# Experts' rows transposed by VectorE and sums fetched by token, in a four-layer kernel

## The chip, the cores and the metric

The kernel runs on one core of one Trainium2 chip, as one launch. The metric is device time in microseconds (us). A core has five engines that run their own instruction queues in order and wait for one another by semaphores: TensorE (PE in the profile: matmuls, with the weight loads shown apart as PEld), VectorE (DVE), ScalarE (ACT), GpSimd (POOL) and SyncE (SP, which here only issues transfers). Transfers run on 16 DMA engines, issued from the queues of SP, ACT and POOL.

## The reference

Two sequences of 1024 tokens, 512 features, all in fp32, pass four blocks, each with a layer norm in front and a residual sum behind: causal attention with 16 heads, a mixture of experts, a state space block, and a feed-forward block whose weights are entries of a table of 16 values.

```python
x = x + _L0_attn_ref(_layernorm(x, axis=-1), ...)
x = x + _L0_ffn_ref(_layernorm(x, axis=-1), ...)      # 32 experts of 192, 8 for a token
x = x + _L1_attn_ref(_layernorm(x, axis=-1), ...)     # state space block
x = x + _L1_ffn_ref(_layernorm(x, axis=-1), ...)      # w = lut[idx], inner size 1376

sel_w, sel_e = jax.lax.top_k(router_logits, TOP_K)
sel_w = jax.nn.softmax(sel_w.astype(jnp.float32), axis=1)
masked = jnp.zeros((T, E), dtype=jnp.float32).at[rows, sel_e].set(sel_w)
...
g = jnp.einsum('th,eih->tei', x, w_gate_proj)
u = jnp.einsum('th,eih->tei', x, w_up_proj)
h = jax.nn.silu(g) * u
h = h * masked_w[:, :, None]
out = jnp.einsum('tei,ehi->th', h, w_down_proj)
```

## The kernel before

Four stretches follow one another: attention (to about 780 us of the profiled span), the experts (to 1520), the state space block (to about 2290) and the feed-forward block.

**Rows and slots.** Beside attention `_Router.route` (L171) normalises blocks of 128 tokens, finds the eight experts of each token and gives each pair of token and expert a slot: each expert has 608 slots (`CAP`), four blocks of 128 and one of 96. `send` (L292) scatters, for one of the eight places and one block, 128 rows of 545 values (`ROW`: 512 features, the token's number, 32 weights) into the DRAM tensor `rows` by an indirect DMA on POOL. The slots are cleared beforehand by SP (`clear`, L400). `acc` is a pair of DRAM tensors in which the sums of tokens grow; the first starts as a copy of the input of the block, and `kept` holds a second copy for the rare case that an expert has no slots left (`_left_over`, L1267, which runs only then).

**Parts.** `_Experts` (L982) goes through the experts from the last to the first, each in two parts: a front part of two blocks (the first sequence) and a back part of three (128, 128, 96 rows). They alternate: front part of expert n, back part of expert n-1. For one part p the method `part` (L1172) writes down the order of TensorE, VectorE and ScalarE by hand (inside `manual_schedule`, L1869, these three engines keep the order of the program):

- `gates(p, 0)` (L1093): four matmuls with the first 128 columns of the expert's weights into a PSUM bank of tag `g`, then SiLU on ScalarE;
- `turn_block(p + 1, 0)` and `(p + 1, 1)` (L1081): for the next part, four TensorE transposes of a block into PSUM (`xg_ps`) and a copy by ScalarE into `xgT`;
- `down(p - 1)` (L1125): the down products of the part before, then ScalarE scales each block's sums by the token's weight into `y` (L1163) and POOL adds them to `acc` by an indirect, accumulating DMA (L1165), whose list of tokens `tok` VectorE copied out of the rows (L1078);
- `gates(p, 1)`, VectorE's product `hT` (L1113);
- `turn_block(p + 1, 2)` for the 96 rows of a back part;
- `gates(p, 2)`, a second SiLU, VectorE's products `hU` (L1121);
- `load_rows(p + 3)` (L1021): SP loads the rows of a later part into `xg`, one row a partition. Such a load waits for the sends that bring its rows.

fp32 matmuls appear as two records each in the profile; a transpose as one.

**Look-up.** Between these steps `rest` (L1217) takes steps of `_look_up` (L904), which turns the table indices of the feed-forward weights into weights in DRAM (`ffn_w`). A piece is 128 x 688 or 128 x 512 indices: SP loads it, ScalarE shortens int32 to bf16 (L927), and for each of the 16 values VectorE makes a mask (L943) and adds mask times value to the sum (L944); SP stores it. It starts at the sixth part.

**The state space block** (`_state_space`, L1347) goes through eight stages of 128 tokens of each sequence. `prepare(st)` (L1382) loads x and both sums from `acc`, adds them (L1393), normalises and transposes. `begin` (L1501) and `products` (L1563) do one chunk step k; POOL makes `xd` (L1528) and `cd` (L1538) for the matmuls of the step after. Outside `manual_schedule` a planner with costs of its own sets the order within each queue.

Of the kernel before, what the change touches and what calls it, by code (L numbers as in the profile page):

```python
# [8 lines left out]
F32 = mybir.dt.float32  # L9
I32 = mybir.dt.int32  # L10
U32 = mybir.dt.uint32
# [34 lines left out]
ROW = D + 1 + E  # L46
# [61 lines left out]

class _Router:
# [8 lines left out]
    def __init__(self, tc, g, x_sb, a, pool, rows, acc, kept, left, ready):  # L118
        nc = tc.nc
        self.tc, self.g, self.x_sb, self.kept = tc, g, x_sb, kept  # L120
        self.pool, self.rows, self.acc, self.left, self.ready = pool, rows, acc, left, ready
# [4 lines left out]
        nc.scalar.dma_start(out=self.wr, in_=a["wr"])  # L126
# [7 lines left out]
        self.number = pool.tile([P, NBLK], I32, tag="number", name="number")  # L134
        nc.gpsimd.iota(self.number, pattern=[[P, NBLK]], base=0, channel_multiplier=1)
# [35 lines left out]
    def route(self, blocks, wk, row_of, bank, apart=False):  # L171
# [12 lines left out]
        for to in (self.acc[0], self.kept):  # L184
            nc.sync.dma_start(
                out=to[b0 * P : (b0 + n) * P, :].rearrange("(n p) d -> p n d", p=P),
                in_=x_sb[:, b0 : b0 + n, :],
            )
# [6 lines left out]
        for i, blk in enumerate(blocks):  # L195
            row = row_of(blk)
            xr.append(row)
            nc.vector.tensor_scalar(
                row[:, :D], x_sb[:, blk, :], mv[:, i, 0:1], rstd[:, i : i + 1],
                ALU.subtract, ALU.mult,  # L200
            )
            nc.gpsimd.tensor_copy(row[:, D : D + 1], self.number[:, blk : blk + 1])
# [74 lines left out]
        for i in range(n):  # L277
            nc.vector.tensor_scalar(
                xr[i][:, D + 1 :], ex[:, i, :], den[:, i : i + 1], None, ALU.mult
            )  # L280
        yield

        nc.vector.tensor_tensor(chosen, chosen, valid, ALU.subtract)  # L283
        miss = wk.tile([P, n, E], F32, tag="miss", name="miss")
        for i in range(n):
            nc.vector.tensor_tensor(miss[:, i, :], chosen[:, i, :], xr[i][:, D + 1 :], ALU.mult)
# [41 lines left out]


def _attention(tc, g, x_sb, a, router, gates, load_gates, make_experts):  # L330


# [11 lines left out]
    rows, acc, ready = router.rows, router.acc, router.ready  # L344
    with ExitStack() as ctx:
# [47 lines left out]

        blank = rp.tile([P, ROW], F32, tag="row", name="blank")
        nc.gpsimd.memset(blank, 0.0)
        nob = wp.tile([P, 1], I32, tag="nob", name="nob")
        nc.gpsimd.iota(nob, pattern=[[0, 1]], base=NT, channel_multiplier=1)
        nc.gpsimd.tensor_copy(blank[:, D : D + 1], nob)

        def clear():  # L400
            for n in range(E * CAPB):
# [1582 lines left out]
```

## Time and profile before

| | us |
|---|---|
| median of 3 runs (2790.9 to 2794.2) | 2792.37 |
| the profiled execution, by the same clock | 2791.15 |
| its span, first to last instruction | 2789.4 |

The profile is of one execution, and its times count from the start of its span. An entry of "busy" is the time in which an engine had an instruction at work; "idle <- X" is what ended the wait before. Some groups of instructions in the experts' stretch, from 830 to 1520 us:

| line | what | count | mean us |
|---|---|---|---|
| L1088 | TensorE transpose of 128x128 | 472 | 0.273 (records overlap) |
| L1091 | ScalarE copy of a transposed block, 128x512 | 118 | 0.591 |
| L1163 | ScalarE scaling of a block's sums, 128x512 | 92 | 0.685 |
| L1165 | POOL, issue of an accumulating scatter | 155 | 1.705 |
| L297 | POOL, issue of a send | 36 | 1.045 |
| L943 | VectorE mask, 128x688 bf16 | 240 | 0.344 |
| L944 | VectorE mask times value plus sum, 128x688 | 240 | 0.936 |
| L927 | ScalarE shortening, 128x688 int32 | 16 | 0.761 |

The 40 slices of the span in tenths of busy time show the stretches (the experts lie in slices 12 to 22):

```
PE   7999999999998899999997899999999999999999
DVE  5555543555236799997774444455455452101100
ACT  1344432443433233333332344444344432101010
POOL 2222220334455533443343010111011010000000
DMA  3366532212479999998885211111111140000000
```

### The profile page before, as it was taken

How to read it: one execution, taken by the hardware profiler on the slowest of the kernel's cores; microseconds unless marked ns; L12 is line 12 of the kernel's file. 1: busy time of each engine (PE TensorE's matmuls, PEld its weight loads, DVE VectorE, ACT ScalarE, POOL GpSimd, SP SyncE). 2: the span in 40 equal slices, each digit the busy share in tenths (PEclk: the TensorE clock that was granted, in tenths of full speed). 3: DMA queues.
4: the chain of work that ended last, by engine and by line, in shares of the span. 5: the costliest groups of instructions: out<-in, count | busy, mean ns of one | idle time of the engine just before them, and what ended most of it. 6: DMA issues, size and time to landing. Idle time of an engine off the chain costs nothing. (4 is left out here: it accounts for less than half of the span.)

```text
span 2789.4 us, 34767 instructions
## 1 busy us (share of the span) xinstructions
PE 2674.8 (96%) x11976; PEld 1616.1 (58%) x11976; DVE 1428.9 (51%) x4016; ACT 925.9 (33%) x1886; POOL 635.4 (23%) x787
## 2 busy tenths in 40 slices
PE   7999999999998899999997899999999999999999
PEld 3444444544465566666664687777777774444444
DVE  5555543555236799997774444455455452101100
ACT  1344432443433233333332344444344432101010
POOL 2222220334455533443343010111011010000000
PEclk9999999999989999999999899999999999999999
DMA  3366532212479999998885211111111140000000
GB/s 116 112 196 188 162 118 76 80 65 82 154 246 251 241 231 256 258 245 200 209 196 93 65 20 43 31 43 43 36 37 49 31 158 15 26 12 23 30 0 27
DMA packets 241257, 311.28 MB, mean 112 GB/s; under 512 B 61264, under 2 KB 129872, under 8 KB 240304
## 3 DMA queue, kind: packets, MB, share of 16 engines
q1 hardware_dynamic: 207808, 232.64, 27.9%
q0 software_dynamic: 32256, 75.58, 12.7%
q8 instruction: 98, 1.61, 0.2%
q10 hardware_dynamic: 1008, 0.73, 0.1%
q14 instruction: 87, 0.71, 0.1%
HBM read 157.93 MB, written 150.95 MB: 111 GB/s over the span
## 5 line engine op out<-in xcount | busy, mean ns | idle before, releaser
L1100 PE MATMUL pg<-xgT,wgu 128*128 128x256 f32 (+1 forms) x1536 | 429.0, 432 | 20.1 <-DVE hT L1113 18.1
L1100 PEld LDWEIGHTS pg<-xgT,wgu 128*128 128x128 f32 x1536 | 289.1, 194 | 149.8 <-issue 56.1
L1165 POOL DMA_INDIRECT acc<-y,tok x160 | 272.0, 1700 | 381.7 <-DMA acc<-y,tok 98.7
L944 DVE SCALAR_TENSOR_TENSOR acc<-hit,lut,acc 128x688 f32<-128x688 bf16 (+2 forms) x405 | 348.8, 861 | 14.4
L1466 PE MATMUL pf<-xT,win 128*128 128x256 f32 x1024 | 245.1, 387 | 9.0 <-ACT gate L1494 4.1
L654 ACT ACTIVATE pT<-st 128x512 f32<-128x512 f32 (+3 forms) x384 | 158.0, 498 | 176.5 <-PE st L641 159.6
L549 PE MATMUL sp<-ka,qa 64*128 64x512 f32 (+3 forms) x768 | 206.9, 510 | 7.5 <-DVE mx L570 4.0
L1466 PEld LDWEIGHTS pf<-xT,win 128*128 128x128 f32 x1024 | 187.8, 191 | 43.0 <-PE pf L1466 7.4
L641 PE MATMUL st<-qa,ka 64*128 64x512 f32 (+3 forms) x768 | 177.3, 500 | 1.5 <-ACT qa L590 1.2
L570 DVE TENSOR_REDUCE mx<-sp 128x1 f32<-128x384 f32 (+3 forms) x352 | 167.3, 491 | 17.9 <-PE sp L549 10.7
L658 POOL TENSOR_SCALAR_AFFINE_SELECT pT<-pT 128x128 f32<-128x128 f32 x256 | 84.1, 341 | 380.6 <-ACT pT L654 369.1
L297 POOL DMA_INDIRECT rows<-row,idx x128 | 128.8, 1007 | 108.3 <-DVE chosen L283 43.6
L1774 PE MATMUL po<-wd,f_hT 128*128 128x512 f32 (+1 forms) x352 | 152.6, 592 | 0.0
L672 PE MATMUL y<-pT,v 128*64 128x512 f32 (+3 forms) x768 | 147.0, 516 | 2.1 <-ACT raw L609 2.0
L549 PEld LDWEIGHTS sp<-ka,qa 64*128 64x128 f32 x768 | 91.7, 186 | 93.5 <-issue 48.8
L1718 DVE TENSOR_TENSOR f_hT<-s,pu 128x512 f32<-128x512 f32 (+1 forms) x37 | 25.4, 687 | 231.4 <-PE pu L1712 231.4
L563 DVE CUSTOM_DVE_ANT_0 junk<-sp,cmask 128x128 f32<-128x128 f32 x256 | 73.2, 286 | 137.3 <-PE sp L549 136.9
L641 PEld LDWEIGHTS st<-qa,ka 64*128 64x128 f32 x768 | 100.1, 188 | 59.6 <-issue 32.4
L1163 ACT ACTIVATE y<-yo,rw 128x512 f32<-128x512 f32 (+1 forms) x128 | 80.8, 682 | 160.3 <-PE yo L1155 160.3
L1712 PE MATMUL pg<-f_xT,wg 128*128 128x512 f32 (+1 forms) x296 | 133.4, 593 | 0.0
L1538 POOL TENSOR_TENSOR cd<-ft_c,ec 128x256 f32<-128x256 f32 x56 | 40.8, 730 | 406.2 <-PE cb L1552 204.9
L1712 PE MATMUL pu<-f_xT,wu 128*128 128x512 f32 (+1 forms) x296 | 133.2, 592 | 0.0
(213 smaller groups left out, 4011.0 us busy)
## 6 DMA issues: line engine op xcount, KB each, us to landing
rows<-blank SPq DMA_DIRECT2D x160, 272.5 KB
xg<-rows SPq DMA_DIRECT2D x64, 545.0 KB
csb<-cs_rows SPq DMA_DIRECT2D x128, 128.0 KB
wgu<-in_wg_dram SPq DMA_DIRECT2D x32, 256.0 KB
wgu<-in_wu_dram SPq DMA_DIRECT2D x32, 256.0 KB
wd<-in_wd_dram SPq DMA_DIRECT2D x32, 256.0 KB
wd<-in_wd_dram SPq DMA_DIRECT2D x64, 128.0 KB
x<-x SPq DMA_DIRECT2D x32, 256.0 KB
```

What stands on the lines that cost most here:

```text
L297: t = tc.nc.gpsimd.indirect_dma_start(out=self.rows[:, :], out_offset=bass.IndirectOffsetOnAxis(ap=idx[:, i, k : k + 1], axis=0), in_=xr[i ...
L549: nc.tensor.matmul(sp[hh][:, c0:c1], lhsT=q[half, pr, tb * P : (tb + 1) * P], rhs=k[half, pr, k0 * P : k1 * P], start=True, stop=True,)
L570: nc.vector.tensor_reduce(m[:, n : n + 1], sp[hh][:, c0:c1], AX.X, ALU.max)
L641: nc.tensor.matmul(st[:, c0:], lhsT=k[half, j // 2, kb * P : (kb + 1) * P], rhs=q[half, j // 2, qt * 512 + c0 : (qt + 1) * 512], start=Tru ...
L654: e = nc.scalar.activation(pT[:, c0:], st[:, c0:], AF.Exp)
L672: nc.tensor.matmul(y[j // 2][half, c0:], lhsT=v[:, kb, h // 2, h % 2 : h % 2 + 2, :].rearrange("p k d -> p (k d)"), rhs=ps[j][:, c0:], sta ...
L944: nc.vector.scalar_tensor_tensor(acc, hit, lut[:n, k : k + 1], acc, ALU.mult, ALU.add)
L1100: nc.tensor.matmul(pg, lhsT=wgu[:, cc, m * P : (m + 1) * P], rhs=xgT[:, cc, :cols], start=cc == 0, stop=cc == NCC - 1,)
L1165: nc.gpsimd.indirect_dma_start(out=self.router.acc[to][:, :], out_offset=bass.IndirectOffsetOnAxis(ap=tok[:m, j : j + 1], axis=0), in_=y[: ...
L1466: nc.tensor.matmul(pf, lhsT=w[wn][:, cc, c0 : c0 + P], rhs=xT[st][:, cc], start=cc == 0, stop=cc == NCC - 1,)
L1712: nc.tensor.matmul(dst[:n, :], lhsT=w[:, cc, fc * P : fc * P + n], rhs=self.xT[tt][:, cc, :], start=cc == 0, stop=cc == NCC - 1,)
L1774: nc.tensor.matmul(po, lhsT=self.hT[tt][fc // 4][:n, fc % 4, j * P : (j + 1) * P], rhs=wd[:n, fc, :], start=fc == 0, stop=fc == NFC - 1,)
```

## The change

**Layout of a row.** A row has 544 values, without the token's number. Its 512 features stand in another order, quarter by quarter: feature c·128 + q·32 + f is stored at q·128 + c·32 + f. The router's weights are loaded in the same order by four transfers.

**Transposes.** `load_rows` brings a part's rows by four transfers, one for each quarter of the features, into 32 partitions each, so that blocks of 32 x 32 lie where VectorE's transpose can turn them into `xgT`. The token's weight for the expert comes by one or two more transfers of single values (`mark`). The gates get four PSUM banks in place of two and two for the transposes.

**Sums.** The scaled sums of a part are stored by SP in the order of the slots (`put`, DRAM tensor `ys`). Each token's eight slots are kept (`slots`), and its sums are fetched by indirect DMAs on POOL (`_collect`), accumulating from the second on: for the state space block's first stage during the last experts, for the second before its first step, for later stages two gathers a chunk step. `acc` is one tensor that is not added to, `kept` is gone.

**Look-up.** A piece is 344 or 256 columns wide. VectorE takes the four bits of the index apart, ScalarE makes eight leaves (the lower or the upper value of each pair of table entries, by the lowest bit), and seven predicated copies on VectorE choose among them by the other bits. Loads and stores of a piece are issued from ScalarE's queue. In each part from the sixth on, eight steps of it are taken: two, three, none and three after the four steps of `part`.

**Order.** The transposes stand after `down`, after `gates(p, 1)` and before `gates(p, 2)`; two places instead of three are sent ahead of the loop, and the third and fourth at its first two parts.

```diff
-ROW = D + 1 + E
+ROW = D + E
...
+def _by_quarter(row):
+    return row[:, :D].rearrange("p (q c f) -> p c q f", q=NQ, f=Q)
...
+        wr = a["wr"].rearrange("(q f) c e -> c f q e", f=Q)
+        for c in range(NCC):
+            nc.scalar.dma_start(out=self.wr[c * Q : (c + 1) * Q], in_=wr[c])
...
-        for to in (self.acc[0], self.kept):
-            nc.sync.dma_start(
-                out=to[b0 * P : (b0 + n) * P, :].rearrange("(n p) d -> p n d", p=P),
-                in_=x_sb[:, b0 : b0 + n, :],
-            )
+        nc.sync.dma_start(
+            out=self.acc[b0 * P : (b0 + n) * P, :].rearrange("(n p) d -> p n d", p=P),
+            in_=x_sb[:, b0 : b0 + n, :],
+        )
...
+                _by_quarter(row), x_sb[:, blk, :].rearrange("p (c q f) -> p c q f", q=NQ, f=Q),
+                mv[:, i, 0:1], rstd[:, i : i + 1], ALU.subtract, ALU.mult,
...
+        nc.vector.tensor_copy(self.slots[:, b0 : b0 + n, :], slot)
...
+        clearing = chain(
+            (rows[r : min(r + P, 1 + E * CAP), :] for r in range(1, 1 + E * CAP, P)),
+            (ys[r : r + P, :] for r in range(0, 1 + (TOPK - 1) * CAP, P)),
+        )
...
-    half = FI // 2
+    most = FI // 4
...
+            for part in range(4):
+                cols = slice(part * most, (part + 1) * most)
+                pieces.append((P, most, a[src][:, cc, cols], ffn_w[dst][:, cc, cols]))
+    for part in range(2):
+        cols = slice(part * D // 2, (part + 1) * D // 2)
+        for fc in range(NFC - 1):
+            pieces.append((P, D // 2, a["didx"][:, fc, cols], ffn_w["wd"][:, fc, cols]))
+        pieces.append((FTAIL, D // 2, a["didx_tail"][:, cols], ffn_w["wd_tail"][:, cols]))
...
-        nc.sync.dma_start(out=idx, in_=src)
+        idx = pool.tile([P, most], I32, tag="idx", name="idx")[:n, :width]
+        nc.scalar.dma_start(out=idx, in_=src)
...
-        short = pool.tile([P, half], BF16, tag="short", name="short", bufs=2)[:n, :width]
+        short = pool.tile([P, most], I16, tag="short", name="short")[:n, :width]
...
+    def store(dst, leaf, bits):
+        nc.scalar.dma_start(out=dst, in_=leaf[0])
+    def merge(leaf, bits, j, k):
+        nc.vector.copy_predicated(leaf[j], bits[k], leaf[j + (1 << k - 1)])
+    more = pool.tile([P, NLUT // 2], F32, tag="more", name="more")
+    pairs = lut.rearrange("p (j k) -> p k j", k=2)
+    nc.vector.tensor_tensor(more, pairs[:, 1], pairs[:, 0], ALU.subtract)
...
+        follows = pieces[i + 1] if i + 1 < len(pieces) else None
+        bits, leaf = [], {}
+        for k in range(4):
+            bit = pool.tile([P, most], I16, tag=f"bit{k}", name="bit", bufs=1 + (k == 3))
+            bits.append(bit[:n, :width])
+            nc.vector.tensor_scalar(
+                bits[k], short, k, 1, ALU.logical_shift_right, ALU.bitwise_and
...
+            )
+        if follows:
+            idx = load(*follows)
+        yield
...
+        def leaves(j):
+            for j in (j, j + 1):
+                tag, bufs = ("leaf", 4) if j else ("acc", 2)
+                leaf[j] = pool.tile([P, most], F32, tag=tag, name=tag, bufs=bufs)[:n, :width]
+                nc.scalar.activation(
+                    leaf[j], bits[0], AF.Identity,
+                    scale=more[:n, j : j + 1], bias=lut[:n, 2 * j : 2 * j + 1],
+                )
+        if done:
+            merge(*done[1:], 0, 3)
+        leaves(0)
+        yield
+        leaves(2)
+        merge(leaf, bits, 0, 1)
+        yield
+        if done:
+            store(*done)
+        merge(leaf, bits, 2, 1)
+        yield
+        leaves(4)
+        merge(leaf, bits, 0, 2)
+        yield
+        leaves(6)
+        merge(leaf, bits, 4, 1)
+        yield
+        if follows:
+            short = shorten(idx, *follows)
+        merge(leaf, bits, 6, 1)
+        yield
+        merge(leaf, bits, 4, 2)
+        yield
+        done = dst, leaf, bits
+    merge(*done[1:], 0, 3)
+    yield
+    store(*done)
...
+def _collect(nc, ys, slots, blk, k, to, add):
+    kw = {"compute_op": ALU.add} if add else {}
+    return nc.gpsimd.indirect_dma_start(
+        out=to, out_offset=None, in_=ys[:, :],
+        in_offset=bass.IndirectOffsetOnAxis(ap=slots[:, blk, k : k + 1], axis=0), **kw,
+    )
...
-        xg = self.wk.tile([P, CAPB - FRONTB, ROW], F32, tag="xg", name="xg", bufs=3)[:, :n]
+        most = CAPB - FRONTB
+        xg = self.wk.tile([P, most * NQ, P], F32, tag="xg", name="xg", bufs=3)
+        mark = self.wk.tile([P, most], F32, tag="mark", name="mark", bufs=5)
...
-        pieces = [(
-            xg[:, : n - back],
-            rows[r : r + (n - back) * P, :].rearrange("(n p) d -> p n d", p=P),
-        )]
+        pieces = [
+            (
+                xg[q * Q : (q + 1) * Q, : m // Q],
+                rows[r : r + m, q * P : (q + 1) * P].rearrange("(t r) d -> r t d", r=Q),
+            )
+            for q in range(NQ)
+        ]
+        c = D + e
+        pieces.append((
+            mark[:, : n - back],
+            rows[r : r + (n - back) * P, c].rearrange("(n p) -> p n", p=P),
+        ))
         if back:
             r += (n - 1) * P
-            pieces.append((xg[:LASTB, n - 1], rows[r : r + LASTB, :]))
+            pieces.append((mark[:LASTB, n - 1 : n], rows[r : r + LASTB, c : c + 1]))
...
+        self.turned[p] = self.wk.tile([P, NCC, most * P], F32, tag="xgT", name="xgT", bufs=2)
...
     def turn_block(self, p, j):
         if p >= len(self.order) or j >= self.blocks(p):
             return
-        nc, xg, xgT = self.tc.nc, self.xg[p], self.turned[p][0]
-        pt = self.bank("t", [P, NCC, P], "xg_ps")
-        m = self.of_block(p, j)
-        for cc in range(NCC):
-            nc.tensor.transpose(
-                pt[:, cc, :m], xg[:m, j, cc * P : (cc + 1) * P], self.g["ident"][:m, :m]
-            )
-        nc.scalar.copy(xgT[:, :, j * P : j * P + m], pt[:, :, :m])
+        xg, xgT = self.xg[p][0], self.turned[p]
+        m = self.of_block(p, j) // Q
+        self.tc.nc.vector.transpose(
+            xgT[:, :, j * P : j * P + m * Q].rearrange("p c (t r) -> p t c r", r=Q),
+            xg[:, j * NQ : j * NQ + m].rearrange("p t (c f) -> p t c f", f=Q),
+        )
...
+        y = self.done[p] = self.wk.tile([P, CAPB - FRONTB, D], F32, tag="y", name="y", bufs=2)
         for j, o in sums:
-            y = self.wk.tile([P, D], F32, tag="y", name="y", bufs=6)
-            to = y.rearrange("p (h d) -> p h d", h=2) if len(o.shape) == 3 else y
             m = self.of_block(p, j)
-            nc.scalar.activation(to[:m], o[:m], AF.Copy, scale=rw[:m, j : j + 1])
-            to = self.turn % 2 if self.both else 1
-            nc.gpsimd.indirect_dma_start(
-                out=self.router.acc[to][:, :],
-                out_offset=bass.IndirectOffsetOnAxis(ap=tok[:m, j : j + 1], axis=0),
-                in_=y[:m], in_offset=None, compute_op=ALU.add,
-            )
-            self.turn += 1
+            to = y[:, j].rearrange("p (h d) -> p h d", h=2) if len(o.shape) == 3 else y[:, j]
+            nc.scalar.activation(to[:m], o[:m], AF.Copy, scale=mark[:m, j : j + 1])
...
+        y, n, back = self.done.pop(p), self.blocks(p), self.order[p][1]
+        r = 1 + self.expert(p) * CAP + back * FRONTB * P
+        pieces = [(
+            self.ys[r : r + (n - back) * P, :].rearrange("(n p) d -> p n d", p=P),
+            y[:, : n - back],
+        )]
+        if back:
+            r += (n - 1) * P
+            pieces.append((self.ys[r : r + LASTB, :], y[:LASTB, n - 1]))
+        for to, src in pieces:
+            t = self.tc.nc.sync.dma_start(out=to, in_=src)
+            self.tc.declare_no_dep(t.ins, group="got", reason="no slots that were read")
+    def collect(self, k, sums):
+        for b in range(B):
+            t = _collect(self.tc.nc, self.ys, self.router.slots, b * TBLK, k, sums[:, b], k > 0)
+            self.tc.add_to_no_dep_group("got", t.ins)
...
         yield
-        for j in range(2):
-            self.turn_block(p + 1, j)
         self.down(p - 1)
+        self.turn_block(p + 1, 0)
         yield
         self.gates(p, 1)
+        self.turn_block(p + 1, 1)
         yield
         self.turn_block(p + 1, 2)
         self.gates(p, 2)
+        self.put(p - 1)
         self.load_rows(p + 3)
         yield
...
             self.banks = {
-                "g": (pool("se_ps_g", 2, PSUM), "g", 2),
-                "t": (pool("se_ps_t", 2, PSUM), "t", 2),
+                "g": (pool("se_ps_g", 4, PSUM), "g", 4),
...
-            for k in range(3):
+            for k in range(2):
...
-                    if i == 0 and not back and n + 1 < TOPK:
-                        send(n + 1)
+                    if i == 0 and (p < 4 or not back) and n + (p > 4) < TOPK:
+                        send(p if p < 4 else n + 1)
                     if p > 4:
-                        for _ in range(1 + back + (i < 1 + (not back))):
+                        for _ in range((2, 3, 0, 3)[i]):
                             next(look_up, None)
+                done, was_back = self.order[p - 1]
+                k = done - (E - TOPK)
+                if was_back and k >= 0:
+                    self.collect(k, sums)
                 if back and n >= TOPK:
                     got = next(fetch, None)
                     if got:
                         _after(tc, got, self.first)
             self.down(len(self.order) - 1)
+            self.put(len(self.order) - 1)
+            self.collect(TOPK - 1, sums)
             for _ in chain(look_up, fetch):
                 pass
...
-            x = xs[st] = xp.tile([P, B, D], F32, tag="x", name="x", bufs=3)
-            part = wk.tile([P, B, D], F32, tag="part", name="part", bufs=1)
+        sums, ys, slots = products_of
+        def collect(st):
+            x = xs[st] = xp.tile([P, B, D], F32, tag="x", name="x", bufs=4)
             for b in range(B):
                 r = slice(block(st, b) * P, (block(st, b) + 1) * P)
-                nc.sync.dma_start(out=x[:, b, :], in_=acc[0][r, :])
-                nc.sync.dma_start(out=part[:, b, :], in_=acc[1][r, :])
+                nc.sync.dma_start(out=x[:, b, :], in_=acc[r, :])
+            if st:
+                for k in range(TOPK):
+                    yield
...
             for b in range(B):
-                nc.vector.tensor_tensor(x[:, b, :], x[:, b, :], part[:, b, :], ALU.add)
+                if st == 0:
...
+        for st in range(2):
+            for _ in collect(st):
+                pass
+        third, gathering = collect(2), iter(())
+        step(third)
...
                     step(out)
+                if c == 2:
+                    step(gathering)
+                    gathering = collect(st + 3) if st + 3 < NST else iter(())
+                step(gathering)
```

## The prediction

> **What bounds the kernel now.** I read the slices of busy time first, then the experts' stretch in finer windows, then the order of instructions inside one expert, then the waits.
>
> ```profile
> span 2789.4 us, 34767 instructions
> PE 2674.8 (96%) x11976; PEld 1616.1 (58%) x11976; DVE 1428.9 (51%) x4016; ACT 925.9 (33%) x1886; POOL 635.4 (23%) x787
> ```
>
> TensorE is busy for 96% of the span, so a gain has to take work off it or close one of its gaps. The experts' stretch (microseconds 836 to 1515 of the span) is where nearly all of the change sits. In windows, with columns PE, weight load, DVE, ACT, POOL, granted clock, DMA share, GB/s:
>
> ```profile
> 836.00:1005.00 169.00, 150.31 (x606) 95.69 (x605) 120.97 (x247) 51.76 (x98) 93.43 (x68) 0.96 0.94 241
> 1005.00:1515.00 510.00, 508.59 (x2158) 331.92 (x2158) 426.15 (x949) 184.02 (x349) 202.34 (x118) 1.00 0.90 215
> ```
>
> Two regimes: until 1005 TensorE idles 19 us and its clock is granted at 0.96; after that it idles 1.4 us in 510. In the second regime the timeline of TensorE repeats every 21.63 us, once for each expert (a front part of 256 rows and a back part of 352):
>
> ```profile
> 1202.62 1.04 PE L1088 MATMUL xg_ps<-ident,xg 128*128 128x128 f32 x8
> 1203.49 1.88 PE L1149 MATMUL yo<-wd,hT 128*128 128x512 f32 x4
> 1205.21 1.03 PE L1149 MATMUL ym<-wd,hT 128*128 128x256 f32 x4
> 1206.17 1.12 PE L1155 MATMUL yo<-wd,hU 64*128 64x512 f32 x4
> 1207.11 0.61 PE L1155 MATMUL ym<-wd,hU 64*128 64x256 f32 x4
> 1207.65 1.99 PE L1100 MATMUL pg<-xgT,wgu 128*128 128x256 f32 x8
> 1209.49 0.50 PE L1088 MATMUL xg_ps<-ident,xg 96*128 96x96 f32 x4
> 1209.82 4.29 PE L1100 MATMUL pg<-xgT,wgu 128*128 128x256 f32 x16
> 1213.94 1.04 PE L1088 MATMUL xg_ps<-ident,xg 128*128 128x128 f32 x8
> 1214.82 1.88 PE L1149 MATMUL yo<-wd,hT 128*128 128x512 f32 x4
> 1216.63 1.13 PE L1155 MATMUL yo<-wd,hU 64*128 64x512 f32 x4
> 1217.69 6.73 PE L1100 MATMUL pg<-xgT,wgu 128*128 128x352 f32 x24
> 1224.25 0.93 PE L1088 MATMUL xg_ps<-ident,xg 128*128 128x128 f32 x7
> ```
>
> Read start to start: the transposes (L1088) hold TensorE for 0.87 + 0.33 + 0.88 = 2.08 us of an expert's 21.63, one gate group of a front part takes 1.84 us, one of a back part 6.56 less one front group, over two: 2.36 us; the down products of a back part 4.16 us, of a front part 2.87. In the first regime the waits of the window 836 to 1010 name the brake:
>
> ```profile
> DVE tok L1078 <- DMA acc<-y,tok: 32.1, 7, 6.4
> POOL acc L1165 <- DMA acc<-y,tok: 17.9, 6, 4.3
> PE pg L1100 <- DVE hT L1113: 16.7, 4, 5.7
> ```
>
> VectorE stands 32 us because a token list (L1078) may not be overwritten before the accumulating scatter that reads it has landed; TensorE then waits for VectorE's product hT.
>
> **The change, part by part.**
>
> *Transposes off TensorE.* Per expert this frees 2.08 us of TensorE, five ScalarE copies (118 of 0.591 us in this stretch, L1091) and four small VectorE copies (0.16 us each, L1077, L1078). It adds five VectorE transposes of 512 values a partition. The trace has none; I price one at 0.69 us, the row x<-x,part (L1393, 128x512 f32, one value a cycle and lane); 0.50 us (L1404, same size, the faster mode) and 1.2 us (two passes) are its ends.
>
> The Trainium skill speaks against this: "VectorE: DVE Perf Modes", section "Rules for kernel authors", gives 128x128 transposes to TensorE where PSUM will do. It judges one transpose, and the trace has TensorE as the full engine here. Followed, the rule would leave the 2.08 us and the time as it was; the rows make a gain possible only while VectorE has room.
>
> *Look-up.* Before, a piece costs VectorE fifteen pairs of hit and multiply-add (0.344 and 0.936 us at 688 wide). After, 54 pieces of 344 (32 of them) or 256 columns, one a part from the sixth part to the 59th: four bit tests, seven predicated copies on VectorE, eight leaves and one shortening on ScalarE, and the two DMA issues move from SP's queue to ScalarE's (0.45 us each by the six ScalarE issues at the start). A bit test: 0.24 us, from hit on 16-bit data (0.344 at 688, 0.291 at 512); 0.42 at most without the fast mode. A predicated copy: 0.52 us, the 0.69 of L1393 less 168 values at 1.04 ns; at least 0.24, at most 0.9 if it needs two cycles a value. A leaf: the int32 shortening gives 0.761 at 688 and 0.613 at 512, so 0.47 at 344; each per-partition operand adds 0.09 (y 0.685 with one, xgT 0.591 without), less 0.05 overlap: 0.60 (0.47 to 0.75). VectorE per expert: 2 x (4 x 0.24 + 7 x 0.52) + 5 x 0.69 + 2.4 for hT and hU = 15 us of 21, from 18. ScalarE: 7.8 (184.02/510 of 21.63) - 2.9 + 9.6 + 1.8 + 0.4 = 17 us, from 8. Both fit, but both are in order, so what decides is the order inside one part.
>
> *The new wait.* ScalarE runs the y copies, then leaves 2 and 3; VectorE merges leaf 2 with leaf 3, merges again, then does hT, then the last two transposes, and only then may TensorE begin the next part's gates. Walk a front part from the end of its down products (a back part's, three y copies): the y copies end at about +1.3 us, two leaves +2.5, two merges +3.55, hT (0.42) +4.0, transposes of a full and a 96-row block +5.2. TensorE meanwhile has two front gate groups, 3.7 us. So it stands 1.5 us. In a back part (two y copies, two gate groups of 2.36, one transpose behind hT) the chain ends at +4.3 against +4.7: no stall. Of 2.08 us freed, 0.57 us an expert remains at 344 columns; at 256 (leaf 0.53, merge 0.43) the stall is 1.2 and 0.85 remains; without look-up all 2.08. Parts 16 to 36: ten experts, -6 us. Parts 37 to 58: eleven, -9. Last five parts: -5. Together **-20 us**.
>
> *Scatter and token lists gone.* The sums are now stored in order of slot by SP (three issues an expert, waiting for y; behind them in SP's queue stand the row loads of three parts ahead, which have 20 us), and POOL no longer accumulates, so L1078's wait and the scatter's own chain go. Parts 4 to 16 took 156.7 us (848.0 to 1004.7). Six experts at the pace just found would take 127. The DMA queues set a second floor. From the packet records of 830 to 1000: 163 of 170 us busy on 16 engines; the 4002 accumulated rows (216 ns each) take 54 of them and become plain stores of about 100 ns, 25 us; the 4608 rows of 2180 bytes at 111 ns become four of 512 bytes at 30 ns, +3 us; their 4-byte marks at 10 to 30 ns, +3 to 9. That is 142, 131 us scaled to 156.7. At 95% busy, 138: **-19 us**. After 1005 the same count gives 18.5 us of DMA an expert, under the 21 of the walk. "DMA: Bandwidth & Descriptors" (section "Specifications") asks for 512 bytes or more a transfer for line rate; the 4-byte marks break it. The 512-byte rows here, at 17 bytes a ns against 20 for 2180, only partly suffer, and no run shows the marks yet.
>
> *Opening parts* (789 to 848): 48 transposes of 0.104 us, not all bound by TensorE: **-3 us** (0 to -6).
>
> *The seam.* Between 1519.6 and 1539.75 TensorE idles 20.1 us: scatter, then load of two sums, then norm. After: last y at 1521.1, two stores issued by 1521.9 and landed by 1524.7 (1.6 us as for dt_rows, and 256 rows x 100 ns / 16), a gather at 1.55 us on POOL and 3.3 to land: 1529.5 against 1534.6 now. **-4 us**, bounds -6 to +2. The extra DMA issues of the router's weights (three of 0.45 us on ScalarE before its table load at 6.13) end before its first norm at 8.83: nothing, and 1 us if that norm came earlier. The kept copy, POOL's row numbers and VectorE's 14 later adds of 0.69 us were hidden behind TensorE (98 to 99% busy there) and give nothing; eight more clearing stores lie in attention, where the DMA engines show 2 to 6 tenths busy.
>
> *Gathers in the state space.* 112 accumulating gathers at 1.55 + 0.3 us on POOL, two a chunk step of about 10 us. Queued behind them are xd and cd, for which TensorE waits. xd is done 3.4 us before use (1766.1 against 1769.5), two gathers take 3.7: nothing if they are issued after xd, 0.3 us in each of 56 steps if before. The second chunk's sixteen stand in one chain of eight, each link 1.85 us issue and 3.3 to 6.4 us landing: 41 to 66 us from 1525. Its features begin 60 us after the seam, but VectorE's norm for it was placed 7 us after the first chunk's; placed so again it would hold VectorE's feature copies and TensorE for up to 30 us. I take 0, bounds -1 and +45.
>
> Sum: -3 - 19 - 20 - 4 = -46. Profiled span 2789.4 becomes 2743; the execution's own time was 2791.15 and the median 2792.37, 3 us above the span, so **2746 us**.
>
> **Rivals.** *The whole gain comes through:* ScalarE's leaves or VectorE's merges are cheaper than priced and no stall stays: -49 for -20, and -30 for -19 as DMA fills up: 2792 - 88 = 2704. For it: both engines have 4 to 6 us free an expert; against: the walk's wait is one of order, not of load. *The seam costs:* the chain of gathers holds VectorE 30 us: 2776. For it: the early place of that norm; against: the need is 60 us away. *VectorE becomes the bound (slower):* merges at two cycles a value (0.9) and transposes in two passes (1.2), bit tests 0.42. Then an expert costs 2 x (1.7 + 6.3) + 6 + 2.4 = 24.4 us: parts 5 to 16 still -10, parts 16 to 36 +28, the narrow ones about +15, the rest -12: 2813. It decides from about 23 us of VectorE an expert. Against it: each is a plain stream of one or two operands. *The change moves no bound:* DMA at 0.94 stays the limit and the pace stays 21.63: only opening and seam gain, 2785; against: 31 us of accumulation leave each 200.
>
> **How the numbers follow.** Forecast 0.50 (its own range 2725 to 2765), whole gain 0.17, seam 0.11, DMA 0.04, VectorE 0.15, and 0.03 for other losses that end near the time before. About 5.6 us (0.2%) is what this kernel's measurement can tell. Faster 0.79, same 0.04, slower 0.17. The range 2703 to 2806 leaves out the worst of the last cases and little below.
>
> **What would show it.** No L1088 on TensorE, and an expert's period of 21.1 us with wide pieces and 20.8 with narrow ones, a gap of 1 to 1.5 us before the gates of each back part, put down to VectorE's transpose; period 19.6 in the last parts. Parts 4 to 16 in 131 to 145 us without waits on the scatter. A seam of 16 us. Wrong if a predicated copy takes over 0.7 us or a transpose over 1 us, if the period is under 20 or over 22 us, if POOL's gathers show up in front of xd, or if DMA stands at 0.98 with TensorE waiting for xg.

## The result and the profile after: 5% slower

The changed kernel takes 2929.3 us (median of 4 runs, 2920.45 to 2931.61), the kernel before 2791.64 us (4 runs beside it): a ratio of 1.0497 with an interval of 1.0478 to 1.0516. Forecast was 2746, and the range ended at 2806. The page's span and busy time after:

```profile
span 2929.4 us, 33627 instructions
...
PE 2642.3 (90%) x11336; PEld 1572.2 (54%) x11336; DVE 1251.2 (43%) x3735; ACT 1084.0 (37%) x2183; POOL 554.9 (19%) x736
```

TensorE has 32.5 us less work, as was meant; its idle time grew from 114.6 to 287.1 us. The timeline of TensorE, cut at its first gate product, the experts' last product and the state space block's first transpose, says where:

| stretch, us | before | after | difference |
|---|---|---|---|
| up to the first gates | 778.0 | 777.6 | -0.4 |
| the experts | 741.6 | 723.9 | -17.7 |
| seam | 20.1 | 20.3 | +0.2 |
| state space block and the rest | 1249.7 | 1407.6 | **+157.9** |

Busy time in windows of the kernel after (columns as in the prediction):

```profile
836.00:1005.00 169.00, 156.64 (x569) 94.28 (x567) 100.58 (x243) 109.52 (x200) 35.51 (x36) 1.00 0.94 266
...
1044.00:1256.00 212.00, 190.24 (x652) 114.36 (x651) 120.30 (x298) 131.99 (x244) 0.00 (x0) 0.94 0.90 233
1256.00:1501.00 245.00, 232.21 (x846) 141.55 (x846) 124.78 (x329) 135.67 (x269) 20.58 (x14) 1.00 0.83 205
...
1522.00:2450.00 928.00, 767.21 (x4588) 582.04 (x4587) 384.26 (x1265) 319.55 (x747) 249.61 (x271) 0.91 0.34 67
```

In the last row TensorE stands idle for 161 of 928 us, and its clock is granted at 0.91, while the DMA engines are busy a third of the time. Before, the block's window had no such hole (18 of 749 us idle):

```profile
1540.00:2289.00 749.00, 731.21 (x4445) 559.22 (x4445) 378.55 (x1245) 312.15 (x732) 77.64 (x155) 0.99 0.16 44
```

The waits of the block after (from 1516 to 2250; total, times, longest):

```profile
...
DVE ln_st L1485 <- DMA x<-ys,slots: 136.1, 14, 24.9
PE pf L1556 <- DVE ft_c L1575: 128.8, 9, 26.1
...
POOL x L1032 <- DMA x<-ys,slots: 85.0, 51, 4.5
```

The fourteen waits in the first line are those of the two halves of a norm (L1485) in the seven stages that fetch their sums. They are uneven: in five stages the norm waited 23 to 25 us, in one 13 and in one 3. The longest on VectorE's timeline:

```profile
1782.86 0.76 DVE L1648 TENSOR_TENSOR wgt<-cb,dec 128x256 f32<-128x256 f32 x2
1808.49 0.69 DVE L1485 BATCH_NORM_STATS2 ln_st<-x 128x6 f32<-128x512 f32 x1 [24.88 <-DMA x<-ys,slots]
1809.10 0.60 DVE L1608 SCALAR_TENSOR_TENSOR dec<-csb,csT,mask 128x128 f32<-128x128 f32 x2
1809.73 0.29 DVE L1575 COPY ft_c<-pf 64x128 f32<-64x128 f32 x1
```

and what TensorE does meanwhile:

```profile
1782.13 1.99 PE L1556 MATMUL pf<-xT,wc 128*128 128x256 f32 x8
...
1784.40 1.89 PE L1556 MATMUL pf<-xT,win 128*128 128x256 f32 x8
1812.36 2.90 PE L1556 MATMUL pf<-xT,win 128*128 128x256 f32 x6 [26.07 <-DVE ft_c L1575]
```

The norm belongs to a stage that is needed a stage (some 120 us) later, but it stands in VectorE's queue in front of this stage's small copies (`ft_c`). They empty the PSUM banks of the feature products, so TensorE stands 26 us. Its next six records take 2.90 us, when eight had taken 1.99. GpSimd's timeline shows what the norm waits for, the gathers (the indirect DMAs that fetch and add a token's sums) of one chain:

```profile
1785.58 1.53 POOL L1032 DMA_INDIRECT x<-ys,slots  x1 [1.21 <-DMA x<-ys,slots]
1786.57 1.30 POOL L1628 TENSOR_TENSOR cd<-ft_c,ec 128x256 f32<-128x256 f32 x1
1790.93 1.57 POOL L1032 DMA_INDIRECT x<-ys,slots  x1 [3.06 <-DMA x<-ys,slots]
...
1806.27 1.53 POOL L1032 DMA_INDIRECT x<-ys,slots  x1 [1.25 <-DMA x<-ys,slots]
...
1807.94 1.33 POOL L1618 TENSOR_TENSOR xd<-bx,dec 128x128 f32<-128x128 f32 x2
```

Sixteen gathers run from 1760 to 1808, each pair waiting for the landing of the one before, because they add to the same rows. `xd` and `cd`, for which TensorE's next step waits, stand between and behind them, eight gathers from one `xd` to the next.

### The profile page after: what moved, and what is told of

It is laid out like the page before. It is cut to its first block, busy times and chain, and to the rows that moved or that the text cites. A ratio compares the mean times of both kernels' runs of the same rounds, so it can differ in the third digit from the quotient of the medians.

```text
span 2929.4 us, 33627 instructions
## 1 busy us (share of the span) xinstructions
PE 2642.3 (90%) x11336; PEld 1572.2 (54%) x11336; DVE 1251.2 (43%) x3735; ACT 1084.0 (37%) x2183; POOL 554.9 (19%) x736
## 5 line engine op out<-in xcount | busy, mean ns | idle before, releaser
L1156 PE MATMUL pg<-xgT,wgu 128*128 128x256 f32 (+1 forms) x1536 | 438.9, 439 | 53.2 <-DVE xgT L1144 29.8
L1556 PE MATMUL pf<-xT,win 128*128 128x256 f32 x1024 | 253.6, 397 | 120.3 <-DVE ft_c L1575 100.0
L970 ACT ACTIVATE leaf<-bit,lut,more 128x344 f32<-128x344 int16 (+2 forms) x378 | 219.4, 636 | 5.1 <-DVE acc L942 3.6
L1032 POOL DMA_INDIRECT x<-ys,slots x112 | 173.4, 1549 | 152.2 <-DMA x<-ys,slots 85.0
L942 DVE COPY_PREDICATED leaf<-bit,leaf 128x344 f32<-128x344 int16 (+2 forms) x216 | 103.2, 505 | 123.2 <-ACT leaf L970 119.6
L1556 PE MATMUL pf<-xT,wc 128*128 128x256 f32 x512 | 124.7, 393 | 34.3 <-DVE ft_c L1575 28.8
L1144 DVE STREAM_TRANSPOSE xgT<-xg 128x512 f32<-128x512 f32 (+1 forms) x160 | 104.7, 671 | 73.8 <-DMA xg<-rows 64.2
```

The lines of the kernel that those rows point to most:

```text
L970: nc.scalar.activation(leaf[j], bits[0], AF.Identity, scale=more[:n, j : j + 1], bias=lut[:n, 2 * j : 2 * j + 1],)
L1032: return nc.gpsimd.indirect_dma_start(out=to, out_offset=None, in_=ys[:, :], in_offset=bass.IndirectOffsetOnAxis(ap=slots[:, blk, k : k + ...
L1156: nc.tensor.matmul(pg, lhsT=wgu[:, cc, m * P : (m + 1) * P], rhs=xgT[:, cc, :cols], start=cc == 0, stop=cc == NCC - 1,)
L1556: nc.tensor.matmul(pf, lhsT=w[wn][:, cc, c0 : c0 + P], rhs=xT[st][:, cc], start=cc == 0, stop=cc == NCC - 1,)
```

## The experiments

Three theories concern the state space block. Theory A: the place of the norm in VectorE's queue makes the loss. Theory B: the traffic of the accumulating gathers does. Theory C: the order of GpSimd's queue does, where the products `xd` and `cd` stand behind gathers. Two concern the experts. Theory D: the DMA engines are the bound from 1044 to 1256. Theory E: the order inside a part makes TensorE wait.

The runs were made in three batches on three chips, and the kernel before took 2786.6, 2804.9 and 2787.7 us in them. So what is given is the ratio of a run to the kernel before of its batch (the change itself: 1.0497), with its interval, and lengths of stretches from each profile. "Block" is the last row of the table above (1249.7 before, 1407.6 after); "experts" its second row (741.6, 723.9). The length of the block hardly depends on the batch: two runs that leave it as in the change have 1408.4 (look-up steps, first batch) and 1408.2 (halves, second batch).

**No gathers.**

```diff
                 for k in range(TOPK):
                     yield
+                    continue
```

> The changed kernel without the 112 gathers of the state space stages 1 to 7; these stages leave the experts' sums out. All theories put the 158 us that the state space gained on these gathers, in one way or another: with them gone the stretch behind the last matmul of the experts should be as long as before the change (1250 us) and the time 2929 - 158 = 2771 us (2764 to 2778). If it stays over 2800, the loss has another cause (order of the features, the x loads).

Ratio 0.9941 (0.9912 to 0.997; median 2773.7, as expected), block 1244.7. The whole loss hangs on the gathers; which of the theories makes it, this run can't say.

**Gathers aside.**

```diff
-                        _collect(nc, ys, slots, block(st, b), k, x[:, b], True)
+                        _collect(nc, ys, slots, block(st, b), k, sums[:, b], k > 0)
```

> The same 112 gathers, issued by GpSimd at the same places, but into the tile sums, which nothing reads between the first stage and the last; stages 1 to 7 leave the experts' sums out. The load on GpSimd's queue and on the DMA engines stays, the wait of VectorE's norm for them goes. Theory A (the norm of a stage was placed on VectorE long before its gathers land, so VectorE and then TensorE stand): 2771 us (2764 to 2785), no wait of VectorE's norm over 2 us. Theory B (the accumulating traffic itself slows the loads and stores of the stages): still 2890 to 2935. Theory C (GpSimd's products xd and cd come late because they are queued behind gathers): still 2890 to 2935, with TensorE waiting for GpSimd.

Ratio 1.0529 (1.0435 to 1.0624): by the words above this would speak against A. The waits (1490 to 2350) show that the run made waits of its own:

```profile
...
DVE dec L1608 <- POOL xd L1618: 82.5, 6, 40.6
...
DVE x L1483 <- DMA sums<-ys,slots: 55.7, 2, 54.4
```

The second stage's gathers stand in the program ahead of the first stage's norm, which reads `sums`: that norm waited 54.4 us. And the gathers, bound to no tile of `x`, were placed early, some seventy ahead of the block's first `xd`. So this run can't separate A from B; what it does show is C's fault in a strong form (`dec` waited 82.5 us for `xd`).

**Norm held.**

```diff
-                nc.vector.bn_stats(stats, x[:, b, :])
+                norm = nc.vector.bn_stats(stats, x[:, b, :])
+                if st:
+                    _after(tc, norm, latest[0], mybir.DependencyClass.NoSync)
...
-                                nc.vector.tensor_copy(dst, src)
+                                latest[0] = nc.vector.tensor_copy(dst, src)
```

(`latest` is also set by the product with the gate, and in the opening the steps of `second` stand after 24 groups of features.)

> The whole computation. The norm of each stage from the second on is tied, by order alone and without a new semaphore, behind the VectorE instruction that stands before it in the program; in the opening of the block the second stage's steps come after 24 groups of features in place of 6. The gathers keep their places. Theory A: VectorE's norm finds its rows there, TensorE does not stand, 2771 to 2790 us, the seam of 20 us unchanged. Theories B and C: the norm's place is a symptom, the time stays over 2880.

Ratio 1.0226 (1.0187 to 1.0264), block 1331.4: 76 of the 158 us are gone, which lies between the two forecasts. No wait of a norm for its gathers is left in the block. Most of the rest is another wait (TensorE, 1505 to 2250, with its cause on GpSimd's timeline):

```profile
PE pf L1560 <- DVE ft_c L1579: 59.5, 7, 13.7
```

```profile
1748.12 1.55 POOL L1032 DMA_INDIRECT x<-ys,slots  x1 [0.33 <-DMA x<-ys,slots]
1751.23 1.54 POOL L1032 DMA_INDIRECT x<-ys,slots  x1 [1.57 <-DMA x<-ys,slots]
1752.22 1.34 POOL L1622 TENSOR_TENSOR xd<-bx,dec 128x128 f32<-128x128 f32 x2
```

`dec` waits for `xd`, `xd` stands behind the eight gathers issued since the `xd` before it, and VectorE's feature copies stand behind `dec`: the same chain, entered from GpSimd.

**Norm held and GpSimd's order; the order alone.** `tc.keep_in_program_order(...)` around the gathers, `xd` and `cd`, so that two gathers follow each step's products.

> The kernel with the norm held, and in addition GpSimd's gathers, xd and cd kept in the order of the program (two gathers after each chunk step's xd and cd, where the planner had put sixteen in a row in four of the stages). The first of the two cost 84 us less than the changed kernel when removed; what was left there were four waits of VectorE's dec for xd of 13.7 us and TensorE behind it. Theories A and C together (two places of one queueing fault, the norm about 85 us and xd about 55 to 70 us): 2771 to 2785 us, no wait for xd over 3 us. Theory B (accumulating traffic): traffic is the same, so 2840 stays.

Ratio 1.0064 (1.0047 to 1.008), block 1279.5. That is short of what A and C together were expected to bring (a block near 1250) and far from what B was (no gain over the norm alone).

> GpSimd's gathers, xd and cd in the order of the program, the norm left to the planner. If the norm's place and the queue of GpSimd are separate faults, this takes off the 55 to 70 us alone: 2860 to 2875. If the norm is the main fault and the gathers now land later (spread over the stage), VectorE waits still longer: 2930 to 3000. If the planner, seeing the gathers late, puts the norm behind them, both faults go: 2770 to 2790.

Ratio 1.017 (1.0136 to 1.0204), block 1317.5. The order alone takes off 90 us, the norm alone 76, both 128. None of the three forms expected for the order alone came: the two faults overlap. With the gathers spread over the stage the norm has less to wait for, 58.1 us in its fourteen waits against 136.1. The same 112 gathers are issued in all these runs, so of the 158 us at least 128 come from places in queues.

**Look-up steps three, two, none, three.**

```diff
-                        for _ in range((2, 3, 0, 3)[i]):
+                        for _ in range((3, 2, 0, 3)[i]):
```

> One edit: the eight look-up steps of a part are taken three, two, none and three in place of two, three, none and three, so that the merge which waits for leaves 2 and 3 (queued on ScalarE behind the copies of y) no longer stands ahead of hT and the transposes on VectorE. Theory E (order inside the part): the wait of 1.4 us ahead of a back part's gates goes, the period of the steady narrow parts falls from 21.2 to 19.7 us; eleven experts there save 16 us, the ten of the stretch from 1044 to 1256 save nothing because the DMA engines hold them: 2929 - 16 = 2913 (2905 to 2918). Rival: the wait only moves to another place of the part, since VectorE or ScalarE are the bound: period 21, 2926 to 2932.

Ratio 1.0419 (1.0349 to 1.0488), experts 694.7, 29 us less than in the profile of the change. (By the ratios it is some 22 us; in the batch's runs with the old steps the experts took 714.9 to 718.5 us.) The wait was this, on TensorE's timeline of the change:

```profile
1309.14 2.60 PE L1156 MATMUL pg<-xgT,wgu 128*128 128x352 f32 x8 [1.41 <-DVE xgT L1144]
```

and on VectorE's, the merge that waits for a leaf, then hT, then the transposes:

```profile
1306.53 0.45 DVE L942 COPY_PREDICATED leaf<-bit,leaf 128x256 f32<-128x256 int16 x1 [0.74 <-ACT leaf L970]
1307.01 0.45 DVE L942 COPY_PREDICATED acc<-bit,leaf 128x256 f32<-128x256 int16 x1
1307.50 0.42 DVE L1169 TENSOR_TENSOR hT<-s,pg 128x256 f32<-128x256 f32 x1
1307.84 1.16 DVE L1144 STREAM_TRANSPOSE xgT<-xg 128x512 f32<-128x512 f32 x2
```

In the new order TensorE runs through a part without a gap:

```profile
1279.05 6.73 PE L1156 MATMUL pg<-xgT,wgu 128*128 128x352 f32 x24
1285.62 1.88 PE L1205 MATMUL yo<-wd,hT 128*128 128x512 f32 x4
```

The period, the time of one expert, falls from 21.17 to 19.71 us in the parts with narrow pieces. The gain is larger than expected since parts before 1044 gained as well (parts 4 to 16 took 125.1 us, 131.2 with the change); from 1044 to 1212 the periods still lie between 21.7 and 24.4 us, as theory D says.

**Weights in halves**, one per back part up to expert 29:

```diff
-                yield nc.sync.dma_start(
-                    out=w[n][:, :, c : c + 512], in_=a[n][:, :, c : c + 512]
-                )
+                for r in range(0, NCC, 2):
+                    yield nc.sync.dma_start(
+                        out=w[n][:, r : r + 2, c : c + 512], in_=a[n][:, r : r + 2, c : c + 512]
+                    )
```

> One edit: the state space weights come in halves of the old pieces, one per back part from expert 8 to 29 (0.5 MB a piece in place of 1 MB, rows of 2 KB as before). Theory D (from 1044 to 1256 the DMA engines are the bound: 21.3 us of packets an expert of which the 1 MB piece is about 3.4 us): with half of it 19.6 us an expert, under the walk's 21.2, so the ten periods of 22 to 24.7 us fall to 21.2 to 22 and the later ones stay 21.2: 2929 - 20 = 2909 (2900 to 2918). Rival: the loads of rows in 512-byte pieces are late for another reason (their place in the queue), then the periods stay where they are and the time at 2925 to 2932.

Ratio 1.0452 (1.0431 to 1.0473). This is the batch in which the kernel before took 2804.9, and the parts before 1000 took 9 us longer here too, so the time itself, 2932.9, can't be held against the forecast; the ratio is 0.0045 under that of the change, some 13 us where 20 were expected. From part 16 to the last one the experts took 499.8 us, against 518.7 in the change's profile and 516.4 and 517.1 in the two profiles of GpSimd's order from the same batch. The periods are the better test: where ten took 22 to 24.7 us, all are at most 21.68, and the later ones stay near 21.17, which is what theory D says and its rival doesn't. In this window (the change: TensorE 190.24 of 212, clock 0.94, DMA 0.90):

```profile
1044.00:1256.00 212.00, 195.13 (x709) 118.00 (x708) 131.15 (x321) 143.41 (x265) 0.00 (x0) 1.00 0.91 232
```

**All four together.**

> Norm held, GpSimd's order, look-up steps three, two, none, three, and the weights in halves, together. From the runs: the state space back to the length of the run without gathers (2771 to 2785), 28 us less by the look-up's order, and up to 15 us less by the spread weights, since at a period of 19.7 us the 19.6 us of packets an expert are at their limit: 2735 us (2715 to 2755), faster than the kernel before by 1.2 to 2.5%. Rival: with the experts' period shorter the DMA engines become the bound over all of them, 2755 to 2775.

Ratio 0.9915 (0.9885 to 0.9944), experts 696.1, block 1276.6: a little faster than before, but less than expected. The forecast of 2735 was reckoned from times of the first batch, where this ratio would be 2763 us: inside the rival's 2755 to 2775. Part of it is the block, 27 us longer than before. In the experts the halves do bring something: from part 16 to the last one they took 486.7 us, 495.6 with the new steps alone. That the whole stretch is no shorter (694.7 without the halves) comes from the parts ahead, which took 10 us longer here. The periods are now 19.7 to 22.7 us through all the parts to expert 29, with the DMA engines at 0.93 from 1044 to 1256.

**The third stage's gathers early**, and the same without gathers:

```diff
         third, gathering = collect(2), iter(())
-        step(third)
+        for _ in third:
+            pass
```

> Norm held, GpSimd's order, look-up steps three, two, none, three (the weights in their old pieces), and the sixteen gathers of the third stage issued in the opening of the state space block, right behind those of the second, where GpSimd stood idle for 48 us in the runs with its order kept. There the third stage's gathers, four a chunk step, still stood in front of xd in the first stage's steps, and TensorE lost some 14 us between 1620 and 1700. Theory C: these go, the block gets 14 us shorter than with norm and order alone (1293 to about 1278 us behind the experts' last matmul), the experts take 690 us as with the look-up's order: 2760 us by a kernel before of 2791 (2750 to 2772), a ratio of 0.985 to 0.993. Rival: VectorE's norm of the second stage waits longer because the accumulating traffic doubles there: 2775 or more.

> The same kernel without the gathers of the stages 1 to 7 (these stages leave the experts' sums out): what the traffic of 112 accumulating gathers still costs when none of them stands in front of anything. Theories A and C (a fault of places alone): 5 to 12 us under the kernel with them. Theory B (the traffic slows the block): 20 us or more under it.

With gathers the ratio is 0.989 (0.9862 to 0.9917; median 2758.8 against 2787.7), block 1267.6: 1.1% faster than the kernel before. 140 of the block's 158 us are now gone with all gathers still issued. Without them the ratio is 0.9844 (0.981 to 0.9878), block 1251.7. So what is left for B is some 16 us, between the two limits; the intervals overlap, so it is a rough figure. TensorE's waits in the block of the first (1505 to 2250):

```profile
PE xn_ps L1506 <- DVE xn L1500: 20.4, 1, 20.4
PE pf L1562 <- DVE ft_x L1581: 10.4, 8, 1.4
```

The first line is the seam; no other wait is long now.

**The kernel before with the new look-up alone** (`_look_up` and its eight steps a part; nothing else of the change):

> The kernel before with the new look-up alone, eight steps a part as in the change; transposes stay on TensorE, sums are scattered as before. VectorE gets about 4 us an expert free, which nothing wants, since TensorE was 98 to 99% busy there; ScalarE, which also copies the transposed blocks, gets 11 us an expert of leaves more and becomes about 19 us of 21.6. Theory (order inside the part): leaves stand ahead of the copies of transposed blocks, TensorE waits 1 to 2 us an expert: +10 to +40 us, slower. Rival: the copies fit between, no change (within 6 us). If the time falls by over 6 us, VectorE was a bound in the kernel before and the change's gain is the look-up's.

Ratio 1.0027 (1.0013 to 1.004), experts 748.7 against 741.6: some 6 us slower, at the limit between theory and rival. The look-up brings no time by itself. What it frees is VectorE, which from 1044 to 1256 is busy for 107.3 us, 195.5 before and 120.3 with the change. That this is the room which the transposes need is an estimate, since no run has them beside the old look-up: at 0.7 us each, five an expert, they would add some 34 us to the 195.5, more than the window's 212.

## Why the prediction was wrong

**The step that failed** is the term "Gathers in the state space", taken at 0 with bounds of -1 and +45. The block became 157.9 us longer. The prediction named both faults and then priced them for an order of the queues that the planner did not set. For the norm, "placed so again it would hold VectorE's feature copies and TensorE for up to 30 us" was said of the second chunk alone. It happened in all seven stages that gather, for 23 to 25 us in five of them: VectorE's norms waited 136.1 us in all, and TensorE 128.8 us for the `ft_c` copies. For GpSimd, two gathers a step were assumed, 3.7 us, behind which `xd` might be 0.3 us late. The planner issued 46 in a row at the block's opening and later put eight between one `xd` and the next. Program order was read as queue order, though this block lies outside the stretch where the order is kept by hand. The rival "The seam costs" (2776) was this mechanism, for one stage of seven, and "if POOL's gathers show up in front of xd" stood among the signs of being wrong.

**Opening parts:** forecast -3, measured -0.4 (58.9 to 58.5 us for the first four parts).

**Scatter gone:** forecast -19 for parts 4 to 16, measured -25.6 (156.8 to 131.2). TensorE's clock was granted at 1.00 there (0.96 before). The floor of 138 us from packet times was too high: at the walk's period of 21.7 us these parts ran with the DMA engines busy for 0.94.

**Transposes, look-up and the new wait:** forecast -20 for parts 16 to 63, measured +8 (510.4 to 518.7). Two terms made the difference of 28 us.

- The larger is the DMA engines' "18.5 us of DMA an expert, under the 21 of the walk". From 1044 to 1256 they were busy for 0.90 of 212 us over nine experts: some 21 us each, with the 512-byte rows at 37 ns (30 taken) and 2048-byte ones at 105. So parts 16 to 37 took 241.1 us, not the 223 or so of the walk. The halves showed it: with the same bytes, spread, the long periods were gone, and parts 16 to 63 took 499.8 us, 19 less.
- The other 9 us are the walk's own wait. It came at the place named, shown by moving one look-up step, and its prices were close: transpose 0.69 and 0.706, predicated copy 0.52 and 0.54, leaf 0.60 and 0.67. But it was longer than counted: the period was 21.67 us with wide pieces (21.1 forecast) and 21.17 with narrow ones (20.8), and without look-up 19.78 (19.6). With wide pieces the transposes' 2.08 us were lost again whole.

**The seam:** forecast -4, measured 0. Its last gather was issued at 1510.2, behind 7.4 us in which GpSimd waited for SP at the branch (L1977), which the sum had left out. VectorE had its rows at 1518.7, 7 us after the issue's end instead of 3.3. Eight loads of x were issued from 1508.5 to 1513.1 beside it; whether they delayed it, no run shows.

**The rivals.** "VectorE becomes the bound" (24.4 us an expert) fell: VectorE was 57% busy from 1044 to 1256. "The change moves no bound" fell as a sum, for the experts did get 17.7 us shorter, but its limit, the DMA engines, is what held the parts from 1044 to 1256. "The whole gain comes through" adds up to 86 us from its own terms (3 + 49 + 30 + 4), not 88.

Some readings in the prediction were off without moving the result. Its 789, 848.0 and 1004.7, and the 830 to 1000 of the packet records, are counted from 11.1 us ahead of the span's start, on which the views count; the lengths are right. The 0.50 us of L1404 is 0.545 by that row's mean, and the seam's stores land at 1525.1 by their own terms (1521.9 + 1.6 + 1.6), not at 1524.7.

The Trainium skill's rule weighed in the prediction ("VectorE: DVE Perf Modes", section "Rules for kernel authors", 128x128 transposes on TensorE) would have kept the old period of 21.63 us. VectorE's transposes give 21.67 and 21.17 in the change as it is, and 19.71 with the steps in the better order. Here the measurement decides against the rule: TensorE was full (210.6 of 212 us busy from 1044 to 1256 before) and VectorE, with the new look-up, was not.

## What to carry to other kernels

Where a planner sets the queues, a new wait has no place until its order is read: ask for each instruction that waits on a transfer where it will stand, how often, and what in order stands behind it. A transfer that is "needed only later" costs its whole latency if its first reader stands early in a busy engine's queue. Tie such a reader behind the work it must not hold up, by order alone, and spread the chain's issues. And when a bound falls, count the next one per period, bursts included: here an average of DMA time under the period hid a stretch in which large pieces held the rows up.

## What the hardware showed that I had not expected

- A wait can cost more than its length. After the gap of 26 us shown above TensorE's matmuls took 0.48 us a record (2.90 / 6) against 0.25 (1.99 / 8), and the clock granted from 1812 to 1817 was 0.50, when it had been 1.00 from 1784.4 to 1786.3. Over the block the mean was 0.91 against 0.99.
- A packet of 512 bytes took 37 ns on its DMA engine in the mean (14 bytes a ns), one of 2048 bytes 105 ns (20 bytes a ns), both from 1044 to 1256 of the change. The Trainium skill ("DMA: Bandwidth & Descriptors", section "Specifications") gives 512 bytes as the least transfer for line rate; here such packets reached 71% of what the longer ones got, and 78% by the medians (27 and 84 ns).
